# A list scheduler that writes four engine queues: scatters spaced on GpSimd, sums of y queued later, fewer zero products ahead of spreads, preparation due later

## The chip, the cores and the metric

The kernel runs on one core of a Trainium2 chip. Its engines are TensorE (PE, matrix products; PEld in the profile is its weight load), VectorE (DVE), ScalarE (ACT), GpSimd (POOL) and SyncE (SP, which only issues DMAs). Each works through its own queue in order; between queues there are only semaphores. GpSimd also issues indirect DMAs (gathers and scatters). The metric is the device time of one execution in microseconds, the median of several runs.

## The reference, cut to what matters

The program is four layers over an image batch of 4 x 64 x 64 x 96. Layers 2 and 3 (attention, an FFT layer and two quantised networks) and the second half of layer 1 are not touched. The work in question is the selective scan of layers 0 and 1. For each image and each of four scan directions, over 4096 positions, 192 channels d and 16 states n:

```python
# L1 (L0 is the same with other scan orders and weights)
x_dbl = einsum('bkdl,kcd->bkcl', xs, x_proj_w)       # dts, B, C
delta = softplus(einsum(dts, dt_projs_w) + dt_projs_b)
A = -exp(A_logs)
def step(h, (x_t, d_t, B_t, C_t)):
    h = h * exp(d_t * A) + (d_t * x_t) * B_t
    y = sum over n of h * C_t
```

In layer 0 the four directions are a diagonal snake, an anti-diagonal snake and two radial orders; in layer 1 they are rows and columns, forwards and backwards. The y of each direction goes back to image order and the four are added.

## The kernel before, in words

The scans of both layers are one stream of eight batches, one per layer and image: four of layer 0, then four of layer 1. A batch has 4 directions (kd) x 4 segments of 1024 positions, 16 segments. Between batches another stage (`side_by_side`) merges the finished image and projects a later one; its own planner is not part of the change. The first-layer norm, the projections and the layers after it stand outside too.

A segment is 24 groups: 6 blocks of 32 channels (cb) times 4 sets of 4 states (sg); a group is a tile of 128 partitions (32 channels x 4 states) x 1024 positions. For a group:

- `spread_u` (L1065, once per block): two products on TensorE copy 32 rows of dtu into all 128 partitions, into the one PSUM buffer u. It waits for the last product t of the block before.
- `load_dt` (L1056, once per block): SP loads dts, 512 KB, the same rows from DRAM, where L1020 has stored them. `load_states` (L1050) loads B and C, eight loads of 512 KB per segment, each into its one place in bc.
- `decay` (L1072): da = exp(dts * A) on ScalarE, four buffers.
- `enter` (L1076): t = u * B on VectorE.
- `recur` (L1083): the scan h on VectorE, four buffers. `keep` (L1094) copies its last column on ScalarE.
- `leave` (L1098): hc = h * C on GpSimd, three buffers.
- `collect` (L1107): TensorE adds hc over the states into y, two products.

VectorE's order is fixed: two products t, two scans h, and so on. After every two blocks y is copied (L1136), turned on TensorE (L1148) and copied into rows (L1152). At the end of a segment the rows are stored: in layer 0, directions 0 and 1, by eight scatters on GpSimd (`store`, L1162), each of 128 rows to scattered rows of the one DRAM tensor y_tok; else by SP. Directions 2 and 3 of layer 0 gather their input on GpSimd (L839); directions 0 and 1 load it in many small diagonal runs on SP (L835), and ScalarE copies it out in as many pieces (L913).

While a segment runs, the next one is prepared (`prepare`): x is turned on TensorE (L897) and copied (L908, L913), projected (L934), biased and split on ScalarE (L947, L949, L951, L953), softplus is made from exp and log (L991 to L1006), and dt is the sum of four terms, made on TensorE as four products with the identity into the one PSUM bank m (L1014), for two halves of the channels times two halves of the positions. ScalarE copies each sum out (L1017), which frees the bank for the next. When a half is complete, SP stores it to DRAM (L1020) and GpSimd multiplies it with x to dtu (L1023). The first spread of a segment needs the first half of dtu, its first decays the first dts load.

The order is written by a planner at build time. `Flow.run` takes the operations (`Op`) of a whole batch, each with an engine, a time on it (`occ`), a latency to users on other engines (`lat`), a due time, and perhaps `hard`. Due times are first lowered so that no user is late. Then it repeatedly takes the operation that can start soonest, and of those within 0.1 us the one with the earliest due time; an operation that isn't hard must not push the engine's next hard one (decay, spread, enter, recur, leave) past its due time by the planner's reckoning, unless its own due time is earlier. A user on the same engine is taken to be ready when the operation before it is done, without `lat`. What it writes is an order alone: on the chip each queue waits for semaphores, not for the planner's times.

When the planner sees a gap on TensorE it calls `keep_busy`, which puts in products with zeros (L1125) that add nothing to an open y:

```python
for _ in range(int((gap - 0.15) * 0.7 / 0.215)):
```

Of the kernel before, what the change touches and what calls it, by code (L numbers as in the profile page):

```python
# [29 lines left out]
SEG = 1024  # L30
# [12 lines left out]
class Kit:  # L43


    def __init__(self, tc, pool):
        self.tc, self.nc = tc, tc.nc
        nc = self.nc
        self.ident = self.t(pool, [128, 128], "ident")
        make_identity(nc, self.ident)  # L50
        self.eps = self.t(pool, [128, 1], "eps")
        nc.vector.memset(self.eps, 1e-5)
# [61 lines left out]
class Op:  # L114


    def __init__(self, engine, occ, emit, deps=(), lat=0.15, due=None, hard=False, bank=0, after=0.0):
        self.engine, self.occ, self.emit, self.lat = engine, occ, emit, lat
        self.deps = [d for d in deps if d is not None]
        self.due, self.hard, self.bank, self.after = due, hard, bank, after  # L120
        self.users, self.left, self.seen = [], 0, 0.0


class Flow:
# [11 lines left out]
    def run(self):  # L136
        inside = set(map(id, self.ops))
        for op in self.ops:
            op.deps = [d for d in op.deps if id(d) in inside]
            op.left = len(op.deps)  # L140
            for d in op.deps:
                d.users.append(op)
        for op in reversed(self.ops):
            for d in op.deps:
                due = op.due - d.occ - (0.0 if d.engine == op.engine else d.lat)
                d.due = due if d.due is None else min(d.due, due)
        free, ready, hard = {}, {}, {}
        for op in self.ops:
            free.setdefault(op.engine, 0.0)
            ready.setdefault(op.engine, [])  # L150
            if op.hard:
                hard.setdefault(op.engine, []).append(op)
        for ops in hard.values():
            ops.sort(key=lambda op: -op.due)
        for op in self.ops:
            if not op.left:
                ready[op.engine].append(op)
        bank, drift, left, strict = 0.0, 0.0, len(self.ops), True
        while left:
            best = None  # L160
            for engine, ops in ready.items():
                if not ops:
                    continue
                first = hard.get(engine, [])
                while first and first[-1].left < 0:
                    first.pop()
                when = lambda op: max(free[engine], op.seen, op.after, bank if op.bank > 0 else 0.0)
                fits = ops
                if strict and first:
                    limit = first[-1].due + drift - (3.2 if engine == "PE" else 0.5)  # L170
                    fits = [
                        op
                        for op in ops
                        if op.hard or op.due <= first[-1].due or when(op) + op.occ <= max(limit, free[engine])
                    ]
                    if not fits:
                        continue
                soonest = min(map(when, fits))
                if soonest == math.inf:
                    continue  # L180
                op = min((op for op in fits if when(op) <= soonest + 0.1), key=lambda op: op.due)
                if best is None or when(op) < best[0]:
                    best = when(op), op
            if best is None:
                assert strict
                strict = False
                continue
            strict = True
            start, op = best
            engine = op.engine  # L190
            if engine == "PE":
                self.fill(start - free[engine])
            op.emit()
            left -= 1
            op.left = -1
            ready[engine].remove(op)
            free[engine] = start + op.occ
            done = start + op.occ
            if op.bank:
                bank = math.inf if op.bank > 0 else done + op.lat  # L200
            if engine == "DVE":
                drift = max(0.0, start - op.due)
            for user in op.users:
                user.seen = max(user.seen, done if user.engine == engine else done + op.lat)
                user.left -= 1
                if not user.left:
                    ready[user.engine].append(user)
        return drift
# [168 lines left out]
class Stream:  # L377
# [493 lines left out]
    def prepare(self, seg, base=0.0, before=None):  # L871
# [3 lines left out]
        ops, o, b = [], seg.o, before.o if before else {}  # L875
# [1 line left out]
        chunks = [slice(j * CH, (j + 1) * CH) for j in range(SEG // CH)]  # L877

        def op(name, engine, occ, emit, deps=(), at=0.0, **kw):
            x = Op(engine, occ, emit, deps, due=base + at, **kw)  # L880
            ops.append(x)
            o[name] = x
            return x

        if seg.i == 0:

            def weights():
                seg.proj = k.t(self.seg, [C, 2, DI + 2 * NS], "proj", bufs=2)
                nc.sync.dma_start(seg.proj, lay.proj[kd])

            op("proj", "SP", 0.1, weights, [b.get(("P", 1, 1))], lat=4.0, at=2.0)
# [23 lines left out]
        for j in range(0, SEG // 128, 2):  # L915
# [5 lines left out]
            if seg.turned:  # L921
                for jj in range(2):
                    occ = 0.19 * len(seg.turned[j + jj]) + 0.25
# [32 lines left out]
        for half in range(2):  # L956
            for j in range(2):
                at = 20.0 + 3.5 * (2 * half + j)
                free = []
                if (half, j) == (0, 0):  # L960
                    free = [b.get(n) for n in (("u", 0), ("u", 1), ("out", 0), ("out", 1), "bc_out", ("sum", 1, 1))]
# [8 lines left out]
                    at=at,  # L970
# [54 lines left out]
        for half in range(2):  # L1025
            for j in range(2):
                at = 48.0 + 4.0 * (2 * half + j)
                for term in range(4):
# [6 lines left out]
                        at=at + 0.9 * term,  # L1035
                        lat=0.3,
# [4 lines left out]
            done = [o["dt", half, 0], o["dt", half, 1]]  # L1041
# [72 lines left out]
            )  # L1114
        self.open = gr if gr.sg < NSG - 1 else None

    def keep_busy(self, gap):


        gr = self.open  # L1120
        if gr is None:
            return
        at = gr.cb % 2 * GC
        for _ in range(int((gap - 0.15) * 0.7 / 0.215)):
            self.nc.tensor.matmul(  # L1125
                gr.seg.y[at : at + GC, :256],
                self.zeros,
                gr.seg.bt.lay.diag.rearrange("p h t c -> p (h t c)")[:, :256],
                start=False,
                stop=False,  # L1130
                tile_position=(0, at),
            )
# [21 lines left out]
    def store(self, seg):  # L1154

        nc, ops = self.nc, []
        rows = lambda: seg.rows.rearrange("p f t d -> p (f t) d")
        to = seg.bt.y_tok[seg.kd]

        def scatter(j):  # L1160
            at = seg.i * (SEG // 128) + j
            nc.gpsimd.indirect_dma_start(  # L1162
                out=to,
                out_offset=bass.IndirectOffsetOnAxis(ap=self.order[:, seg.kd, at : at + 1], axis=0),
                in_=rows()[:, j, :],
                in_offset=None,
            )

        def whole():
            at = self.start(seg)  # L1170
            dst = to[at : at + SEG, :].rearrange("(f p t) d -> p f (t d)", f=2, t=4)
            nc.sync.dma_start(dst, seg.rows.rearrange("p f t d -> p f (t d)"))

        def columns(w):
            nc.sync.dma_start(self.by_columns(to, seg, w), rows()[w * HW : (w + 1) * HW])

        if seg.bt.lay.ordered and seg.kd < 2:
            return [Op("POOL", 1.25, partial(scatter, j), lat=4.0) for j in range(SEG // 128)]
        if seg.bt.lay.ordered or seg.kd % 2 == 0:
            return [Op("SP", 0.1, whole, lat=4.0)]  # L1180
        return [Op("SP", 0.1, partial(columns, w), lat=4.0) for w in range(2)]
# [568 lines left out]
class Ffn:  # L1750
# [20 lines left out]
    def __call__(self, xs, store):  # L1771

        nc, take, give = self.k.nc, self.rings.take, self.rings.give
        xq = yield from take(self.work, [C, 4, CH], "xq", 2, F8)
        xm = yield from take(self.work, [C, 4, CH], "ln_xm", 1)
        read = []

        def out(j, rs):
            nc.vector.tensor_tensor(xq[:, j], xm[:, j], rs, ALU.mult, saturate=False)
            self.plan.add(self.layers(xq, j, xs[j], store, read))  # L1780

        yield from self.norm(xs, [xm[:, j] for j in range(4)], out)
        give(xm)
        del xm

    def layers(self, xq, j, x, store, read):
        nc, work, take, give = self.k.nc, self.work, self.rings.take, self.rings.give
        hq = yield from take(work, [128, 3, CH], "hq", 3, F8)
# [599 lines left out]
```

## Time and profile before

| | |
|---|---|
| median of 3 runs | 15374.65 us (15372.34 to 15387.42) |
| profiled execution | 15402.95 us, span 15401.2 us |
| mean granted clock of TensorE | 0.937 |
| eight scan batches | 386 to 1736, 1948 to 3279, 3492 to 4829, 5054 to 6380 us (layer 0); 6589 to 7891, 8051 to 9344, 9500 to 10801, 10900 to 12194 us (layer 1) |
| scans h, VectorE (L1083) | 2304 of 2355 ns and 768 of 2287 ns |
| products t, VectorE (L1076) | 3072 of 1239 ns |
| products hc, GpSimd (L1098) | 3072 of 2365 ns |
| decays, ScalarE (L1072) | 3072 of 1151 ns |
| zero products, TensorE (L1125) | 7824 records (two passes each), 1986.3 us |
| scatters, GpSimd (L1162) | 256 of 997 ns |

The page's first part gives busy time, share and instruction count of each engine over the whole span. A window view gives the same for a stretch of time, with the clock that was granted to TensorE as a share of full speed. A wait line reads: engine and line that stood idle, what it waited for; us in total, times, the longest. A timeline line starts with the start and the length in us. A product of f32 with 512 columns stands in the trace as two passes.

### The profile page before, as it was taken

What the parts mean: (1) busy time and instruction counts of PE and PEld (TensorE: products, weight loads), DVE (VectorE), ACT (ScalarE), POOL (GpSimd) and SP (SyncE); (2) the same over time, 40 slices, a digit from 0 to 9 for tenths busy, and PEclk for the clock granted to TensorE, in tenths of its full rate; (3) what the DMA queues carried; (4) which work ended last, traced back from release to release, by engine and by line L of the source; (5) the groups of instructions that cost most, each with busy time, mean ns of one, the idle gap of its engine ahead of it and who ended that gap; (6) DMA issues with size and microseconds to landing.
All of it is one profiled execution on the core that took longest, in us unless ns stands there. A gap on an engine that the chain in (4) does not pass through costs nothing. (4 is left out here: it accounts for less than half of the span.)

```text
span 15401.2 us, 196660 instructions
## 1 busy us (share of the span) xinstructions
PE 13827.4 (90%) x74369; PEld 5096.1 (33%) x74369; DVE 12827.4 (83%) x9642; ACT 8327.7 (54%) x13421; POOL 9203.3 (60%) x4657
## 2 busy tenths in 40 slices
PE   8899899989998999899989998999899789998877
PEld 3233333333333333333333333333233244443344
DVE  1999799978997899799979997999899856555655
ACT  3666466646664666466656665666566423232333
POOL 0788678867886688667747774777577620000123
PEclk9999899989998999899989999999999999998888
DMA  2333433343334333433343334333433400000122
GB/s 67 117 113 125 150 111 111 126 148 112 111 127 146 106 118 128 148 116 117 123 152 124 118 124 152 126 118 120 156 119 120 142 10 11 19 15 12 52 72 71
DMA packets 662768, 1637.49 MB, mean 106 GB/s; under 512 B 102822, under 2 KB 268460, under 8 KB 658045
## 3 DMA queue, kind: packets, MB, share of 16 engines
q1 hardware_dynamic: 624956, 1549.37, 31.4%
q0 software_dynamic: 36864, 75.55, 1.7%
q8 instruction: 588, 9.63, 0.3%
q14 instruction: 360, 2.94, 0.1%
HBM read 1295.03 MB, written 329.58 MB: 105 GB/s over the span
## 5 line engine op out<-in xcount | busy, mean ns | idle before, releaser
L1098 POOL TENSOR_TENSOR hc<-h,bc 128x1024 f32<-128x1024 f32 x3072 | 7198.4, 2365 | 2216.1 <-DVE h L1083 1909.0
L1083 DVE TENSOR_TENSOR_SCAN h<-da,state,t 128x1024 f32<-128x1024 f32 x2304 | 5300.4, 2355 | 26.0 <-ACT state L1094 16.3
L1072 ACT ACTIVATE da<-dts,L_A_logs 128x1024 f32<-128x1024 f32 x3072 | 3520.0, 1151 | 1832.2 <-DVE h L1083 1786.7
L1076 DVE TENSOR_TENSOR t<-u,bc 128x1024 f32<-128x1024 f32 x3072 | 3629.8, 1239 | 267.6 <-PE u L1065 193.5
L1107 PE MATMUL y<-hc,gather_y 128*32 128x512 f32 x12288 | 3529.1, 620 | 311.9 <-POOL hc L1098 241.7
L1125 PE MATMUL y<-L_diag,zeros 96*32 96x256 f32 x7824 | 1986.3, 386 | 0.0
L1083 DVE TENSOR_TENSOR_SCAN h<-da,t 128x1024 f32<-128x1024 f32 x768 | 1717.4, 2287 | 17.3 <-ACT da L1072 9.1
L1065 PE MATMUL u<-dtu,spread 32*128 32x512 f32 x3072 | 1573.1, 632 | 120.0 <-DVE t L1076 109.2
L1125 PEld LDWEIGHTS y<-L_diag,zeros 96*32 96x32 f32 x7824 | 852.8, 111 | 1425.0 <-issue 926.1
L1107 PEld LDWEIGHTS y<-hc,gather_y 128*32 128x32 f32 x12288 | 595.8, 109 | 2021.1 <-issue 1029.1
L934 PE MATMUL m<-xs,proj 96*128 96x512 f32 (+1 forms) x2048 | 1070.2, 641 | 67.3 <-ACT spare L1152 32.5
L1642 DVE SCALAR_TENSOR_TENSOR hcv<-padv,taps,hcv 128x2048 f32<-128x2048 f32 x384 | 902.2, 2350 | 13.4
L1566 POOL MEMSET padp<- 128x2448 f32 x32 | 68.6, 2143 | 1400.8 <-PE d L1606 1378.3
L1023 POOL TENSOR_TENSOR dtu<-dt,xs 96x1024 f32<-96x1024 f32 x256 | 603.0, 2356 | 506.1 <-ACT dt L1017 501.1
L1606 PE MATMUL d<-padp,diag 32*32 32x512 f32 x25600 | 885.7, 601 | 2.0 <-ACT hcp L1621 2.0
L1065 PEld LDWEIGHTS u<-dtu,spread 32*128 32x128 f32 x3072 | 521.4, 188 | 943.6 <-issue 588.0
L1017 ACT COPY dt<-m 96x512 f32<-96x512 f32 x512 | 297.2, 580 | 694.5 <-PE m L1014 690.0
L1014 PE MATMUL m<-dtu,ident 96*96 96x512 f32 x1024 | 563.8, 632 | 72.7 <-ACT dt L1017 65.9
L1606 PEld LDWEIGHTS d<-padp,diag 32*32 32x32 f32 x25600 | 484.4, 103 | 369.8 <-issue 196.9
L934 PEld LDWEIGHTS m<-xs,proj 96*128 96x128 f32 (+1 forms) x2048 | 324.6, 181 | 770.6 <-issue 483.8
L947 ACT ACTIVATE sp_z<-m,L_dtb 96x512 f32<-96x512 f32 x512 | 350.0, 684 | 409.5 <-PE m L934 393.5
L1014 PE MATMUL m<-sp_log,ident 96*96 96x512 f32 x1024 | 539.2, 608 | 0.0
(275 smaller groups left out, 15495.8 us busy)
## 6 DMA issues: line engine op xcount, KB each, us to landing
bc<-bc_dram SPq DMA_DIRECT2D x1024, 512.0 KB
dts<-dt_dram SPq DMA_DIRECT2D x768, 512.0 KB
dt_dram<-dt SPq DMA_DIRECT2D x256, 384.0 KB
y_tok<-spare SPq DMA_DIRECT2D x64, 768.0 KB
dt<-y_tok SPq DMA_DIRECT2D x128, 384.0 KB
x_tok<-y_rows SPq DMA_DIRECT2D x32, 768.0 KB
z_t<-z_rows SPq DMA_DIRECT2D x64, 384.0 KB
dx<-x_tok SPq DMA_DIRECT2D x64, 384.0 KB
```

Source lines behind the costliest of these rows:

```text
L934: nc.tensor.matmul(v.ps, seg.proj[:, src, to], seg.xs[:, src, chunks[j]], start=src == 0, stop=src == 1)
L1014: nc.tensor.matmul(v.ps, k.ident[:C, :C], term[:, half, chunks[j]], start=at == 0, stop=at == 3)
L1023: nc.gpsimd.tensor_mul(seg.dtu[:, half], v.dt[:, half], seg.xs[:, half])
L1065: self.nc.tensor.matmul(seg.u[:, cols], self.spread[rows, :], seg.dtu[rows, half, cols], start=True, stop=True)
L1072: self.nc.scalar.activation(gr.da, gr.seg.dts[gr.cb], AF.Exp, scale=scale)
L1076: self.nc.vector.tensor_mul(gr.t, gr.seg.u, self.bc[:, 0, gr.sg, :])
L1083: self.nc.vector.tensor_tensor_scan(gr.h[:, order], gr.da[:, order], gr.t[:, order], start, op0=ALU.mult, op1=ALU.add)
L1098: self.nc.gpsimd.tensor_mul(gr.hc, gr.h, self.bc[:, 1, gr.sg, :])
L1107: nc.tensor.matmul(seg.y[at : at + GC, :], self.gather_y, gr.hc[:, part * CH : (part + 1) * CH], start=gr.sg == 0, stop=gr.sg == NSG - 1, ...
L1125: self.nc.tensor.matmul(gr.seg.y[at : at + GC, :256], self.zeros, gr.seg.bt.lay.diag.rearrange("p h t c -> p (h t c)")[:, :256], start=Fal ...
L1606: nc.tensor.matmul(pc[i][j * 32 : (j + 1) * 32, :], diag[mine, ON_PE.index(t), tap, :], pad[mine, j * 8 + dy : j * 8 + dy + 8, dx : dx + H ...
L1642: nc.vector.scalar_tensor_tensor(to, win, wt, to, op0=ALU.mult, op1=ALU.add)
```

## The change

Five edits to the planner and what it is given; no operation is added or taken away but zero products.

1. Scatters: each now depends on the one before it and is marked `lands`: a user on the same engine also counts its latency, now 3.0 us (4.0 before).
2. Sums later: in the planner a user on TensorE of an operation on GpSimd (a `collect` of a `leave`) is ready 1.0 us later.
3. Zero products: ahead of a hard operation of TensorE (a spread), a gap is filled with a share of 0.35; ahead of others 0.7 as before.
4. Preparation: every operation of `prepare` is due 18.0 us later.
5. `keep_busy` takes the share.

```diff
-        self.users, self.left, self.seen = [], 0, 0.0
+        self.users, self.left, self.seen, self.lands = [], 0, 0.0, False
...
-                self.fill(start - free[engine])
+                self.fill(start - free[engine], 0.35 if op.hard else 0.7)
...
             for user in op.users:
-                user.seen = max(user.seen, done if user.engine == engine else done + op.lat)
+                pad = 1.0 if (engine, user.engine) == ("POOL", "PE") else 0.0
+                near = user.engine == engine and not op.lands
+                user.seen = max(user.seen, done if near else done + op.lat + pad)
...
         def op(name, engine, occ, emit, deps=(), at=0.0, **kw):
-            x = Op(engine, occ, emit, deps, due=base + at, **kw)
+            x = Op(engine, occ, emit, deps, due=base + at + 18.0, **kw)
...
-    def keep_busy(self, gap):
+    def keep_busy(self, gap, share):
...
-        for _ in range(int((gap - 0.15) * 0.7 / 0.215)):
+        for _ in range(int((gap - 0.15) * share / 0.215)):
...
         if seg.bt.lay.ordered and seg.kd < 2:
-            return [Op("POOL", 1.25, partial(scatter, j), lat=4.0) for j in range(SEG // 128)]
+            ops = []
+            for j in range(SEG // 128):
+                ops.append(Op("POOL", 1.25, partial(scatter, j), ops[-1:], lat=3.0))
+                ops[-1].lands = True
+            return ops
```

## The prediction

> **What bounds the kernel now.** I read the page first (one core, so no second die), then the engines' busy time in the eight scan batches, then VectorE's waits there, and last the timelines around single waits.
>
> ```profile
> PE 13827.4 (90%) x74369; PEld 5096.1 (33%) x74369; DVE 12827.4 (83%) x9642; ACT 8327.7 (54%) x13421; POOL 9203.3 (60%) x4657
> ```
>
> No engine is full over the whole span. The share is a mean over stages, so the scan batches have to be cut out. The windows below are the batches, four of layer 0 and four of layer 1; columns are us of window, busy us of each engine (instructions), granted clock, DMA.
>
> ```profile
> core 0: us, PE busy (x) PEld busy (x) DVE busy (x) ACT busy (x) POOL busy (x), PEclk, DMA share, GB/s
> 386.00:1736.00 1350.00, 1245.75 (x4070) 406.85 (x4070) 1291.53 (x768) 854.04 (x1498) 1097.32 (x543) 0.95 0.35 116
> 1948.00:3279.00 1331.00, 1235.68 (x4074) 404.73 (x4074) 1290.97 (x768) 851.57 (x1495) 1097.32 (x543) 0.96 0.35 115
> 3492.00:4829.00 1337.00, 1239.37 (x4074) 406.20 (x4072) 1291.04 (x768) 851.18 (x1495) 1097.51 (x543) 0.96 0.35 115
> 5054.00:6380.00 1326.00, 1225.71 (x4069) 400.69 (x4068) 1290.48 (x768) 849.20 (x1447) 1097.47 (x544) 0.97 0.35 116
> 6589.00:7891.00 1302.00, 1223.16 (x4102) 401.15 (x4099) 1289.99 (x768) 836.63 (x1211) 971.11 (x415) 0.98 0.36 118
> 8051.00:9344.00 1293.00, 1208.43 (x4099) 397.69 (x4098) 1287.73 (x768) 840.69 (x1214) 970.76 (x415) 0.99 0.37 119
> 9500.00:10801.00 1301.00, 1216.18 (x4102) 399.98 (x4102) 1289.10 (x768) 841.09 (x1215) 970.56 (x415) 0.98 0.36 118
> 10900.00:12194.00 1294.00, 1202.33 (x4124) 399.76 (x4124) 1287.96 (x768) 819.81 (x1186) 965.81 (x413) 0.99 0.36 117
> ```
>
> Here VectorE is the bound: 1288 to 1292 us of products and scans in every batch. Window minus VectorE busy is 58.5, 40.0, 46.0 and 35.5 us in layer 0 and 12.0, 5.3, 11.9 and 6.0 in layer 1: **215 us, all that this change can win**. The same subtraction over the first segment of each batch gives 44.6 us, a start-up the change hardly touches; 171 us are left. Outside the batches the diff changes no order.
>
> The waits say who holds VectorE up (total us, times, longest):
>
> ```profile
> POOL y_tok L1162 <- DMA y_tok<-spare,scan_idx: 123.5, 60, 4.6
> ...
> DVE t L1076 <- PE u L1065: 193.5, 123, 7.0
> ```
>
> VectorE's product t waits for the spread u on TensorE. Of the late spreads, those of layer 0 that stand right behind zero products or sums of y cost 83 us and those behind the last dt sum (L1014) 57 us; in layer 1 nearly all (26 of 29 us) stand behind zero products. The scatter's wait starts many of them: GpSimd stands 4.4 us behind its own scatter, the sums of y behind it stand, TensorE idles, and then its clock drops:
>
> ```profile
> 2047.10:2050.50 3.40, 2.50 (x7) 0.57 (x4) 3.40 (x3) 3.38 (x6) 0.00 (x0) 1.00 0.41 107
> 2050.50:2053.90 3.40, 1.98 (x4) 0.66 (x4) 3.40 (x3) 3.37 (x6) 2.84 (x2) 1.00 0.24 66
> 2053.90:2060.70 6.80, 5.84 (x11) 1.30 (x12) 6.80 (x5) 3.23 (x4) 4.96 (x5) 0.50 0.31 105
> ```
>
> Sorting TensorE's idle stretches in the batches by length: of 37 of 2.0 us or more, 35 were followed within 3.4 us by half clock, for about 7 us; of 756 under 1.5 us, 44 were.
>
> **The change part by part.** Instruction counts stay the same on every engine but TensorE.
>
> *Scatters.* In the old order 72 of the 224 follow-up scatters stand directly behind the one before and 4 behind one product; in the new order every one stands behind exactly two products hc, 2 x 2.365 = 4.73 us. A scatter lands 2.4 us (median) to 4.9 us (95%) after its issue, 1.0 of which is the issue itself. So the 123.5 us of GpSimd waiting go. It is off the bound; its worth is in the late spreads.
>
> *Sums later.* The added 1.0 us exists only in the planner. In the order, 95 of 96 spreads per batch now have four groups' sums still to come behind them (before: 47 in layer 0, 18 in layer 1; the others had three). A spread no longer stands behind the newest product of GpSimd. Who waits for that: hc has three buffers, so GpSimd may wait for a sum (108 us in all now); it has 1331 - 1097 = 234 us of slack a batch, so I put it at nothing.
>
> *Zero products.* 3912 become 3014; the 1004 right ahead of spreads go, 106 come elsewhere. 898 x 2 passes x 0.215 us = 386 us less on TensorE, none of it on the bound. The two ahead of a spread took 0.86 us; without them TensorE idles that long, which by the count above costs the clock seldom.
>
> I take these three to remove all 171 us. The bounds: 83 (only those behind zero products and sums in layer 0) and 171.
>
> *Preparation later.* This adds a wait. The dt sums of the next segment move from about 20 us ahead of its start to just ahead of its first spread: on TensorE the last four-term sum now stands directly, or with one sum of y between, in front of that spread. On ScalarE, at 12 of 15 boundaries in a layer-0 batch and 7 of 15 in layer 1, the first decay of the next segment now stands in front of the dt copy that frees the only PSUM bank m for that last sum. This decay needs the dts load; the load needs the dt store. The planner counts the load's 4.5 us but no time from the store to the load, since both are on SP. The trace does:
>
> ```profile
> SPq L1056 <- DMA dt_dram<-dt: 298.0, 117, 4.5
> ```
> ```profile
> 2515.24 0.31 SPq L1020 DMA_DIRECT2D dt_dram<-dt  x1
> 2518.32 0.51 SPq L1056 DMA_DIRECT2D dts<-dt_dram  x1
> ```
>
> In 16 such pairs: copy to store 0.03, store to load 3.08, load to its landing (semaphore increments in the trace) 3.65, together 6.8 us.
>
> The walk, in us before the moment at which VectorE could start the next segment (twelve pairs of groups, 6.735 us each, make the 80.8 us of a segment, 1293 / 16): the last spread's release, the end of the second product t of the tenth pair of groups, is at -(3 x 6.735 - 2.34) = -17.9 (two products take 2.34 in the timeline). Boundary A (24 in layer 0, 28 in layer 1): spread 1.72, a sum of y 0.9, one dt term 0.86, so -14.4; ScalarE is in a decay until -14.2; copy 0.58: -13.6; store and load 6.8: -6.8; decay 1.15 (row L1072): -5.7; copy 0.58: -5.1; four terms in eight passes 0.43 us apart, 3.5: -1.6; spread 1.98: +0.4. So 0.4 us late, and TensorE idles about 2.5 us before the last sum. Boundary B (segments 2 to 7 of a layer-0 batch, 24): all four terms follow the spread, so the copy ends at -11.2 and the first product is 2.8 us late; two bc loads of 512 KB stand right ahead of the store, worth 0 to 2 us more: I take 3.8, and 3 to 5 us of idle TensorE.
>
> Idle of that length brought half clock in 35 of 37 cases. Its price: the 1331 us batch at clock 0.96 has 8% of 1331 = 106 us of half clock and 40 us of idle VectorE, 0.38 us per us, so 2.6 us per stretch of 6.8 us. A: 0.4 + 0.9 x 2.6 = 2.7, x 52 = 140 us. B: 3.8 + 2.6 = 6.4, x 24 = 154 us. Bounds for both together: 0 (the copy is early enough) and 24 x 8.1 + 52 x 4 = 402 us.
>
> The Trainium skill, TensorE: Matmul & The Clock Gate, Part 1, says that the clock falls after at least one idle window of about 3.4 us. By that rule idle of 2.5 us at A would cost no clock, and the sum would be -171 + 52 x 0.4 + 154 = +4 us, an estimate; the 35 of 37 above speak against it.
>
> **Sum.** -171 + 140 + 154 = +123 us. The profiled run took 15402.95 (span 15401.2 and 1.8 around it), 28 above the median 15374.65, so 15526 there and **15498** as a median.
>
> **Rivals.** *1, faster:* the late preparation is hidden. If the first dt copy comes 1 us earlier than in my walk at A and 3.8 at B, the spread is ready in time and nothing pays for the 171 us. For it: 0.4 us at A is no more than a walk can miss. Against it: the walk gives the queues no delay of their own, and B is far off. With 0 to 40 us paid: 15205 to 15245. *2, in between:* the boundary waits come, but the clock holds: 52 x 0.4 + 24 x 3.8 = 112, minus 171 = -59: 15316; with half of the stretches at half clock (92 us more) 15408. Against it: the 35 of 37. *3, the change does not do what it says:* within a segment spreads stay late behind x turns and projections that wait for ScalarE; only 83 of 171 go: 15586. Against it: in segments 10 to 14 of layer 0 the same projections stand there and VectorE has at most 1 us of idle time in each.
>
> **How the numbers follow.** Forecast 0.46 (own range 15420 to 15590, 78 us below for A or B mis-sized, 92 above), rival 1 0.25, rival 2 0.18, rival 3 0.11. A measurement of this kernel tells about 0.2% (31 us) from no change. Of rival 2 I put 0.10 faster and 0.08 within 0.2%; two hundredths of the forecast lie there too. So faster 0.35, same 0.10, slower 0.55. The range runs from 15225, the middle of rival 1, to 15600, just past rival 3.
>
> **What would show it.** Right: scatter waits near zero on GpSimd; t waiting for u inside segments nearly gone; new waits of t for u at the first product of a segment, 2 to 8 us, with decay waiting for the dts load on ScalarE (now 2 times, then some 70) and the clock at 0.5 there; layer-1 batches slower than their 1293 to 1302 us. Wrong: decays never wait for dts, or wait and the clock stays full; then it is rival 1 or 2.

## The result, and the profile after

The changed kernel takes 15499.83 us (median of 7 runs, 15451.88 to 15516.9) against 15387.42 us of the kernel before in the same runs (15363.73 to 15415.73): 1.0068 times as long, 95% interval 1.0052 to 1.0083. Forecast were 15498 us, 123 us more than the median that the kernel before had at that time (15374.65); measured beside each other it is 112 us more. The total is right; several of the terms behind it are not, as the experiments show.

The profiled execution has a span of 15483.8 us and a mean granted clock of 0.910 (before: 15401.2 us and 0.937). The page's first part:

```profile
PE 13814.7 (89%) x72573; PEld 4962.3 (32%) x72573; DVE 12833.7 (83%) x9642; ACT 8282.6 (53%) x13421; POOL 9212.5 (59%) x4657
```

VectorE is as busy as before (12827.4 us), TensorE has 1796 instructions fewer. The eight scan batches, columns as in the prediction (us of window, busy us of each engine, granted clock, DMA):

```profile
core 0: us, PE busy (x) PEld busy (x) DVE busy (x) ACT busy (x) POOL busy (x), PEclk, DMA share, GB/s
373.00:1733.00 1360.00, 1235.13 (x3874) 390.73 (x3874) 1289.53 (x768) 850.82 (x1497) 1095.89 (x542) 0.92 0.34 115
1940.00:3296.00 1356.00, 1236.97 (x3881) 392.41 (x3882) 1289.81 (x768) 847.23 (x1494) 1096.43 (x542) 0.93 0.33 113
3500.00:4859.00 1359.00, 1238.50 (x3881) 392.99 (x3882) 1289.65 (x768) 847.13 (x1494) 1096.21 (x542) 0.93 0.33 113
5067.00:6423.00 1356.00, 1242.96 (x3877) 391.75 (x3876) 1289.80 (x768) 844.22 (x1446) 1095.72 (x542) 0.92 0.34 113
6626.00:7937.00 1311.00, 1226.77 (x3837) 382.01 (x3838) 1290.24 (x768) 827.13 (x1210) 967.36 (x413) 0.93 0.36 117
8097.00:9407.00 1310.00, 1219.19 (x3841) 381.52 (x3840) 1289.79 (x768) 833.28 (x1215) 968.80 (x414) 0.93 0.36 117
9565.00:10865.00 1300.00, 1210.70 (x3841) 379.51 (x3840) 1289.48 (x768) 833.33 (x1215) 969.00 (x414) 0.94 0.36 118
10970.00:12271.00 1301.00, 1207.28 (x3871) 383.32 (x3870) 1288.85 (x768) 812.55 (x1186) 966.56 (x413) 0.94 0.35 116
```

Window minus VectorE busy, added up, is 336 us; before it was 215. Sorted by place in the trace, some 306 us of it lie at the first product t of a segment (258 in layer 0, 48 in layer 1), 15 us in the first segments of the batches, 12 us inside the other segments. The layer-0 batches are all 1356 to 1360 us long (1326 to 1350 before): idle time has left the segments and gathered at their boundaries. The waits (us in total, times, longest), first one line of the kernel before, then the changed kernel:

```profile
ACT da L1072 <- DMA dts<-dt_dram: 32.2, 2, 30.0
```

```profile
DVE t L1078 <- PE u L1067: 348.8, 121, 11.2
ACT da L1074 <- DMA dts<-dt_dram: 340.6, 74, 30.2
```

The line of GpSimd waiting for its scatter (123.5 us before) is gone from the list. VectorE waits for the spread 348.8 us in place of 193.5, and the decay waits for the dts load 74 times in place of 2. One boundary of kind B, from the timeline (start, us, engine, line, operation; idle before it and what ended that):

```profile
2184.80 0.58 ACT L1019 COPY dt<-m 96x512 f32<-96x512 f32 x1 [1.68 <-PE m L1016]
2185.40 0.32 SPq L1022 DMA_DIRECT2D dt_dram<-dt  x1
...
2190.67 1.16 SPq L1058 DMA_DIRECT2D dts<-dt_dram  x2
...
2194.61 1.15 ACT L1074 ACTIVATE da<-dts,L_A_logs 128x1024 f32<-128x1024 f32 x1 [5.79 <-DMA dts<-dt_dram]
2195.66 0.56 ACT L1019 COPY dt<-m 96x512 f32<-96x512 f32 x1
...
2196.28 2.02 PE L1016 MATMUL m<-dtu,ident 96*96 96x512 f32 x2 [4.29 <-ACT dt L1019]
...
2201.18 1.02 PE L1016 MATMUL m<-sp_log,ident 96*96 96x512 f32 x2
...
2202.13 1.98 PE L1067 MATMUL u<-dtu,spread 32*128 32x512 f32 x4
...
2204.15 2.36 DVE L1078 TENSOR_TENSOR t<-u,bc 128x1024 f32<-128x1024 f32 x2 [8.81 <-PE u L1067]
```

It is the chain of the walk: copy, store, load, decay, the copy that frees bank m, the last dt sum, the spread, the product t. ScalarE stands 5.79 us at the decay with the copy behind it; TensorE then starts the sum after 4.29 us of idle time and needs 5.85 us from its start to the spread's.

```profile
2194.60:2198.00 3.40, 1.72 (x2) 0.68 (x3) 0.73 (x1) 3.39 (x4) 1.01 (x1) 0.50 0.90 341
```

The clock in that stretch is 0.50.

### The profile page after: what moved, and what is told of

Same layout as the page of the kernel before. It is cut to its first block, busy times and chain, and to the rows that moved or that the text cites. A ratio compares the mean times of both kernels' runs of the same rounds, so it can differ in the third digit from the quotient of the medians.

```text
span 15483.8 us, 192971 instructions
## 1 busy us (share of the span) xinstructions
PE 13814.7 (89%) x72573; PEld 4962.3 (32%) x72573; DVE 12833.7 (83%) x9642; ACT 8282.6 (53%) x13421; POOL 9212.5 (59%) x4657
## 5 line engine op out<-in xcount | busy, mean ns | idle before, releaser
L1078 DVE TENSOR_TENSOR t<-u,bc 128x1024 f32<-128x1024 f32 x3072 | 3595.2, 1216 | 422.8 <-PE u L1067 348.8
L1109 PE MATMUL y<-hc,gather_y 128*32 128x512 f32 x12288 | 3786.3, 664 | 28.4 <-POOL hc L1100 28.4
L1067 PE MATMUL u<-dtu,spread 32*128 32x512 f32 x3072 | 1659.7, 662 | 419.4 <-DVE t L1078 412.2
L1127 PE MATMUL y<-L_diag,zeros 96*32 96x256 f32 x6028 | 1508.1, 384 | 0.0
L1109 PEld LDWEIGHTS y<-hc,gather_y 128*32 128x32 f32 x12288 | 667.3, 114 | 1904.3 <-issue 1482.2
L1127 PEld LDWEIGHTS y<-L_diag,zeros 96*32 96x32 f32 x6028 | 620.4, 110 | 1011.0 <-issue 602.2
L1016 PE MATMUL m<-dt,ident 96*96 96x512 f32 x1024 | 556.4, 626 | 0.0
```

Source lines behind the costliest of these rows:

```text
L1016: nc.tensor.matmul(v.ps, k.ident[:C, :C], term[:, half, chunks[j]], start=at == 0, stop=at == 3)
L1067: self.nc.tensor.matmul(seg.u[:, cols], self.spread[rows, :], seg.dtu[rows, half, cols], start=True, stop=True)
L1078: self.nc.vector.tensor_mul(gr.t, gr.seg.u, self.bc[:, 0, gr.sg, :])
L1109: nc.tensor.matmul(seg.y[at : at + GC, :], self.gather_y, gr.hc[:, part * CH : (part + 1) * CH], start=gr.sg == 0, stop=gr.sg == NSG - 1, ...
L1127: self.nc.tensor.matmul(gr.seg.y[at : at + GC, :256], self.zeros, gr.seg.bt.lay.diag.rearrange("p h t c -> p (h t c)")[:, :256], start=Fal ...
```

## The experiments

The runs below were made on three other chips, four kernels at a time, each set beside its own runs of the kernel before (medians 15259.77, 15257.82 and 15262.07 us). The kernel before is thus about 127 us faster there than above. Times are compared as ratios within one chip; where two chips are set against each other it is said.

### The two kernels again, on one chip (e5, e6)

> The changed kernel itself, so that it stands beside the kernel before and the next kernels on one chip. Ratio to the kernel before 1.0052 to 1.0083 as measured, so +80 to +125 us; boundary waits of 280 to 310 us in all.

> The kernel before, for its profile on the same chip. If the 127 us by which it was faster on the chip of the first experiments lie between the scan batches, the eight batches add up to 10535 us within 20 and the stretches between them to 1120 to 1275 us, by the chip. If they lie in the batches, its late spreads cost less than 193.5 us there, and the 171 us that could be won were fewer on that chip.

The changed kernel: 15396.8 us, ratio 1.0084 (1.0071 to 1.0098), 139 us slower, a little more than the 80 to 125 expected; its boundary waits are 294 us. The kernel before: 15280.04 us in its one run. Its batches add up to 10566.4 us (10535.0 in the first profile, so 31 more and not within 20), and the seven stretches between them to 1118.8 us in place of 1273.3. So the 127 us lie between the batches (the single profiled run of e6 is itself 22 us above the median): each of the four stretches up to the first layer-1 batch takes about 175 us in place of 209 to 225. The changed kernel shows the same difference, a smaller one (179 to 185 here, 203 to 208 on the first chip). Why one chip does this work more slowly was not looked at. The idle time that could be won is there on this chip too: 245 us by the windows.

The two traces on this chip also show a cost of the change outside the scan windows. Of the 111 us between the two profiled runs 69 lie in the batches (10635.4 against 10566.4) and 38 in the seven stretches between them (1156.9 against 1118.8). With the later preparation dt sums for the next batch stand among the last instructions of a batch: the last turn of y ends 8 to 12 us after the last scan in place of 5 to 6, and VectorE starts on the merge after 16 to 22 us in place of 13 to 16, 28 us over the seven. (In e1 below, without the later preparation, it is 13 to 16 us as before.) On the first chip VectorE's start is late in the same way (23 us over the seven), but there the stretches as a whole were 26 us shorter than before.

### Without the later preparation (e1)

```diff
-            x = Op(engine, occ, emit, deps, due=base + at + 18.0, **kw)
+            x = Op(engine, occ, emit, deps, due=base + at, **kw)
```

> The changed kernel with the preparation due as before; scatters, sums of y and zero products as changed. Theory: these three remove the waits of t for u (193.5 us in the kernel before) and add no boundary wait, so 130 to 175 us faster than the kernel before (15210 to 15255 us, ratio 0.9885 to 0.9915), layer-0 batches near 1290 to 1300 us. Rival (they reach only the spreads behind zeros and sums of layer 0): about 83 us faster (15300). Rival (the boundary waits of the changed kernel come from the later sums or the missing zero products, not from the preparation): no faster than before.

15203.88 us, ratio 0.9965 (0.9953 to 0.9977): 56 us faster, not 130 to 175, and less than the rival's 83. There is no boundary wait to speak of (37 us), so the third reading falls. The late spreads sorted by what stands directly ahead of them on TensorE, against e6: behind zero products 85 us in layer 0 and 43 in layer 1 become none; behind the last dt sum of layer 0 61 become 59; behind sums of y, turns and projections, in both layers, 8 become 52. The scatters, the later sums and the zero products do not clear the segments by themselves. The late spreads behind the dt sums are still there, and they are not there in the changed kernel: it is the later preparation that takes the dt sums out of the segments and puts their wait at the boundary.

### Each of the three alone (e9, e10, e11)

Each is the kernel before with one edit of the change: the scatters' dependence and `lands`; the 1.0 us from GpSimd to TensorE; the share of 0.35.

> The kernel before with the scatters spaced apart and nothing else. Theory: GpSimd's waits for its own scatters (107 to 124 us) go, and with them the late spreads of the layer-0 segments in which scatters stand; 15 to 50 us faster, layer 1 (no scatters) within 20 us of before. Rival (the scatter's wait is hidden by GpSimd's slack): within 15 us of before although the waits are gone.

> The kernel before with the sums of y queued 1 us later and nothing else. Theory: a spread no longer stands behind the newest product of GpSimd, so the late spreads behind zero products get fewer in both layers (85 us in layer 0 and 43 in layer 1 on the chip of e6): 20 to 60 us faster; those behind the last dt sum (61 us) stay. Rival: the sums behind the spread are late instead and hold the next one, within 15 us of before.

> The kernel before with a share of 0.35 ahead of spreads and nothing else. Theory: two zero products fewer, 0.86 us, ahead of some 80 late spreads, so 20 to 60 us faster; half clock rises from some 640 to over 1000 us in the eight batches and costs nothing, since it falls where VectorE does not wait. If half clock had its price of 0.38 us per us, the kernel would be 100 us or more slower.

| kernel | median, us | ratio (95% interval) | t waits for u, us | half clock in the batches, us: layer 0, layer 1 |
|---|---|---|---|---|
| before (e6) | 15257.82 | 1 | 224.6 | 436, 204 |
| scatters alone (e9) | 15132.33 | 0.9919 (0.9905 to 0.9933) | 104.3 | 224, 170 |
| sums later alone (e10) | 15270.5 | 1.0007 (0.9998 to 1.0016) | 185.8 | 665, 718 |
| zero products alone (e11) | 15270.86 | 1.0007 (0.9998 to 1.0015) | 205.0 | 521, 394 |
| the three together (e1) | 15203.88 | 0.9965 (0.9953 to 0.9977) | 142.8 | 658, 700 |

The theory missed in all three, and at e10 the rival held. (At e11 half clock rose to 915 us and not to over 1000, and cost nothing that can be seen, as its theory had it: at 0.38 us per us the 275 us more would have been 105 us.) **The scatters alone give 130 us**, two and a half times the upper end that I gave them, and the other two give nothing alone and take away 74 us of the 130 when they are added (0.9919 to 0.9965, two chips). Windows of the second and third batch, first the kernel before (e6), then the scatters alone:

```profile
1903.00:3245.00 1342.00, 1244.26 (x4073) 406.14 (x4071) 1290.95 (x768) 849.57 (x1495) 1096.33 (x543) 0.96 0.34 114
3420.00:4761.00 1341.00, 1243.56 (x4077) 405.72 (x4078) 1291.04 (x768) 849.86 (x1495) 1096.91 (x544) 0.96 0.35 114
```

```profile
1876.00:3176.00 1300.00, 1226.99 (x4142) 406.01 (x4140) 1288.80 (x768) 850.40 (x1495) 1098.19 (x544) 0.98 0.36 118
3350.00:4650.00 1300.00, 1227.53 (x4145) 406.43 (x4144) 1288.83 (x768) 850.46 (x1495) 1097.66 (x543) 0.98 0.36 118
```

Forty us of VectorE's idle time go from each batch. In the waits, the line of e6 below has no counterpart in the run with the scatters alone:

```profile
POOL y_tok L1162 <- DMA y_tok<-spare,scan_idx: 107.4, 53, 4.6
```

The late spreads behind the last dt sum of layer 0 fall from 61 to 12 us, those behind zero products there from 85 to 23. The edit does not touch the dt sums, but a scatter that takes longer in the planner's timetable changes what it writes for the other engines. Ahead of the fifth spread of segment 2 of a layer-0 batch, TensorE's order is

```
before:         y, 7 zeros, y, 4 zeros, y, dt sum, dt sum, spread
scatters alone: y, 6 zeros, y, 3 zeros, dt sum, y, dt sum, spread
three together: y, y, 7 zeros, y, 3 zeros, dt sum, y, dt sum, spread
```

Is it the scatter's wait that made the spreads late, as the forecast had it, or this order? In segments 1 to 5 of the layer-0 batches (counted from 0) both changed, and 90 us of late spreads become none. In segments 6 and 7 TensorE's order stayed word for word; GpSimd's waits for its scatters (2 us in each) went, and the late spreads did not: 16.5 us before, 19.5 after; those behind the last dt sum of segment 6 are 1.51 to 1.52 us late in all four batches of both runs. And among the 20 segments 1 to 5 there are five in which GpSimd waited under 2 us for scatters in e6; late spreads cost 3.4 us in the mean in each of these, 4.9 in each of the other 15. By that some 68 of the 90 us (20 x 3.4) come from the order and 22 from the wait, an estimate; no run kept the order and took the wait away in these segments.

The later sums alone (e10) clear the spreads behind zero products in both layers (85 and 43 us to 0), and some 87 us return behind dt sums (61 to 88 in layer 0), sums of y, turns and projections. In the order with the three together, above, four sums of y stand between the two spreads and not three: the one that no longer stands ahead of the spread before has to be done as well. e1 has that order and no waits at scatters, and its dt sums are late by 59 us. That the fourth sum is the cause is argued from the order, not shown by a run that moves it alone. GpSimd's waits for sums of y, which the forecast put at nothing, rose too (hc has three buffers): from 115 us in e6 to 237 in e10 and 280 in e1. Whether any of that reaches VectorE was not tried.

The half clock stands against the price that I had put on it. Layer-1 windows, e6 and then e10:

```profile
6442.00:7742.00 1300.00, 1218.52 (x4102) 400.07 (x4099) 1289.53 (x768) 835.62 (x1211) 970.79 (x416) 0.98 0.36 118
7901.00:9205.00 1304.00, 1219.89 (x4103) 400.59 (x4102) 1289.47 (x768) 839.63 (x1215) 970.15 (x415) 0.98 0.36 118
```

```profile
6448.00:7741.00 1293.00, 1190.60 (x3720) 368.22 (x3718) 1289.63 (x768) 825.00 (x1211) 970.82 (x415) 0.93 0.37 118
7900.00:9194.00 1294.00, 1185.98 (x3716) 367.45 (x3716) 1288.86 (x768) 829.54 (x1214) 971.02 (x416) 0.94 0.37 119
```

The clock falls from 0.98 to 0.93 and the batches get shorter. Over the layer, 514 us more at half clock (718 against 204) go with 21 us less time (5189.3 against 5210.6). At 0.38 us per us they would have cost 195 us. VectorE's whole idle time in these four batches of e10 is 31 us, so 718 us at half clock can have cost no more than that.

### The later preparation alone (e2)

```diff
-            x = Op(engine, occ, emit, deps, due=base + at, **kw)
+            x = Op(engine, occ, emit, deps, due=base + at + 18.0, **kw)
```

> The kernel before with the preparation due 18 us later and nothing else. In its order the first decay of the next segment stands ahead of two dt copies at the boundaries into segments 1 to 8 of a layer-0 batch (32 in all), at none or one in the rest. Theory: each of these 32 costs what the changed kernel pays there, 7 to 10 us (mean 9 into segments 2 to 7), and the 57 us behind the last dt sum inside segments go: 32 x 8.5 - 57 = 215 us slower than before (15600), layer 1 within 20 us of before. Rival (the wait needs the other parts too): between -57 and 0 us against before.

15329.78 us, ratio 1.0052 (1.0038 to 1.0065): 70 us slower, a third of what I expected; layer 1 is as forecast (5170 us against 5211 in e6). In layer 0 (5427 against 5356) decays do wait for the dts load (174.7 us, 32 times, in place of 32.5, 2 times), but the first products t of the segments wait only 22 us: in this order the last dt sum stands behind the first spread of the segment, and it is the spread of the second half of the channels, 40 us into the segment, that comes late, by up to 9.2 us and 133 us in all. So the wait does not need the other parts, but where it falls and how large it is depends on them.

### The store seen by the planner (e3)

```diff
-            op(("out", half), "SP", 0.1, partial(out, half), done, at=60.0, lat=3.0)
+            op(("out", half), "SP", 0.1, partial(out, half), done, at=60.0, lat=3.0).lands = True
...
-                due = op.due - d.occ - (0.0 if d.engine == op.engine else d.lat)
+                due = op.due - d.occ - (0.0 if d.engine == op.engine and not d.lands else d.lat)
```

> The changed kernel, but the planner counts 3.0 us from the dt store to the dts load; then only the last dt copy, which nothing of the next segment waits for but dtu's second half, stands behind the decay. Theory (the decay that waits for the dts load holds the copy that frees bank m): the boundary waits nearly all go, 306 us of VectorE idle time down to under 60, so 250 to 290 us faster than the changed kernel and 140 to 180 us faster than before (15205 to 15250 us); t waits for u less than 80 us in all. Rival (the late dt sums are late by themselves, whatever stands on ScalarE): within 60 us of the changed kernel (15440 or more).

15213.04 us, ratio 0.9971 (0.996 to 0.9982): 47 us faster than before. Against the changed kernel (1.0084 on another chip) that is 1.1%, some 170 us, where 250 to 290 were expected and the rival had at most 60. The boundary waits fall from 294 (e5) to 119 us:

```profile
DVE t L1078 <- PE u L1067: 160.9, 84, 7.0
ACT da L1074 <- DMA dts<-dt_dram: 150.8, 67, 29.0
```

Decays still wait 67 times, but of the dt copies at most the last stands behind them, and no dt sum ahead of the spread waits for that one; most of their waiting costs nothing. Nor did the preparation simply move earlier: at the boundaries of kind B the store is issued 9.1 us before VectorE is free, in the changed kernel (e5) 9.2 us before, and yet the last dt sum starts 2.6 us before that moment in place of 0.8 us after it, and takes 3.8 us in place of 5.5. That shows the copy behind the decay to be the cause of the larger part. Of the 119 us left, 76 are at the 24 boundaries of kind B, 3.2 each: there four dt sums go through one bank, each behind the copy of the one before, and end up to 3 us after VectorE is free (1.2 in the mean). This part of the rival is true.

### The clock at the boundary (e4)

```diff
             if at == 0:
+                if (half, j) == (1, 1) and lay.ordered and 2 <= kd * NSEG + seg.i < 8:
+                    self.zeros_here(before, 8)
                 v.ps = k.t(self.ps, [C, CH], "m")
```

`zeros_here` puts eight products with zeros into the y that the segment before has still open (the sum of y before it keeps it open for them).

> The changed kernel with eight more zero products (3.9 us at full clock) in TensorE's idle time ahead of the last dt sum, at the boundaries into segments 2 to 7 of the layer-0 batches (24). The decay, the copy and the order stay. There TensorE stood idle 2 to 5 us, then went through the last sum at half clock, 6.9 us for eight passes that take 3.5 at full clock. Theory: the clock holds and each boundary gets 2 to 3.4 us cheaper, 50 to 80 us faster than the changed kernel, waits of 4 to 6 us stay. Rival (the wait alone counts, the half clock is only seen with it): within 20 us of the changed kernel. If the zero products run late, in place of idle time that is no longer there: up to 50 us slower.

15350.34 us, ratio 1.0063 (1.0049 to 1.0077); the changed kernel has 1.0084 on another chip, so about 32 us less, between the theory and the rival; the two intervals overlap, so the times alone don't prove a gain. The traces say it more sharply. The same boundary as above:

```profile
2172.67 1.15 ACT L1076 ACTIVATE da<-dts,L_A_logs 128x1024 f32<-128x1024 f32 x1 [5.93 <-DMA dts<-dt_dram]
...
2174.34 1.10 PE L1018 MATMUL m<-dtu,ident 96*96 96x512 f32 x2 [0.56 <-ACT dt L1021]
...
2176.99 1.02 PE L1018 MATMUL m<-sp_log,ident 96*96 96x512 f32 x2
...
2177.94 1.98 PE L1069 MATMUL u<-dtu,spread 32*128 32x512 f32 x4
...
2179.96 2.36 DVE L1080 TENSOR_TENSOR t<-u,bc 128x1024 f32<-128x1024 f32 x2 [6.71 <-PE u L1069]
```

The decay waits as long as before (5.93 us), TensorE idles 0.56 us in place of 4.29, and from the sum's start to the spread's it takes 3.60 us in place of 5.85. Over the 24 boundaries of kind B the last sum takes 3.60 us in place of 5.49 (e5), it starts 0.5 us later behind the zeros, and the product t is 6.94 us late in place of 8.34. None of the 24 sums runs into half clock any more (20 in e5). So the clock's share of the wait at B is 1.4 us of 8.3, 34 us in all; the rest is the chain itself.

### Less late, and the copy seen too (e7, e8, e12)

e7 and e8 are e3 with 12 and 6 us in place of 18; e12 is e7 with

```diff
-                op(("dt", half, j), "ACT", 0.5, partial(keep_dt, half, j), [p], at=at + 4.0, bank=-1)
+                op(("dt", half, j), "ACT", 0.5, partial(keep_dt, half, j), [p], at=at + 4.0, bank=-1, lat=1.5)
```

> Store latency seen by the planner as in e3, preparation due 12 us later in place of 18. In its order the last dt sum stands four to six instructions ahead of the first spread, and two of the three remaining copies behind a decay are gone. Theory (with the copy free of the decay, the 76 us left at the boundaries into segments 2 to 7 are the chain of four dt sums through one bank, simply too late): 6 us earlier takes most of them, the inside of the segments stays quiet: 30 to 80 us faster than e3, so 75 to 130 us faster than before. Rival (earlier sums are late inside the segment again, as in e1): equal to e1 or e3, 40 to 60 us faster than before.

> The same with 6 us. No dt copy stands behind a decay of the next segment; the last sum stands seven to eleven instructions ahead of the first spread. Theory: no boundary wait, but the last sums come near the last spread inside the segment, 13.5 us ahead of the boundary: 50 to 110 us faster than before, on either side of e7. Rival (the in-segment waits behind the last sum come back in full): 40 to 60 us faster than before, as e1.

> e7 (store latency seen, preparation due 12 us later), and the planner counts 1.5 us in place of 0.15 from a dt copy to its users, among them the next dt sum, which needs the bank. In e7 most late spreads stand behind the second term of a dt sum that waited for that copy on ScalarE (64 us). Theory: they fall to under 30 us and no boundary wait comes back: 20 to 60 us faster than e7, so 90 to 130 us faster than before. Rival (the sums then stand as a whole ahead of the spread and are late just the same): within 20 us of e7.

| kernel | median, us | ratio (95% interval) | boundary waits, us | late spreads behind dt sums, us |
|---|---|---|---|---|
| 18 us, store seen (e3) | 15213.04 | 0.9971 (0.996 to 0.9982) | 119 | 95 |
| 12 us (e7) | 15189.69 | 0.9954 (0.9942 to 0.9966) | 0 | 116 |
| 6 us (e8) | 15285.93 | 1.0016 (1.0005 to 1.0026) | 14 | 171 |
| 12 us, copy seen (e12) | 15125.83 | 0.9918 (0.9903 to 0.9933) | 6 | 49 |

(The last column counts those at the boundary too.) With 12 us no boundary wait is left, as expected, but the sums come late inside the segment: 68 us faster than before, not 75 to 130. With 6 us they fall ahead of a spread inside the segment in both layers, and all the gain is gone; the rival had put it at 40 to 60 us faster. Counting the copy's real delay (e12) gives 136 us, a little above the 90 to 130 expected: the late spreads behind the second term of a dt sum, 64 us of layer 0 in e7, fell to 3, those behind dt sums of any kind from 116 to 49. e12 and the scatters alone are the fastest kernels of the study, within their intervals equal, and both beat the two kernels of this case. Their edits can be joined; that was not run.

## Why the prediction was right, point by point

**The bound and what was to be seen** were as forecast. VectorE's busy time did not move (1289 to 1290 us a batch). The scatter waits are gone, waits of t for u inside the segments too (12 us), the new ones stand at the first product of a segment, decays wait for the dts load 74 times (some 70 forecast), and three of the four layer-1 batches are 7 to 17 us longer (the other is 1 us shorter). VectorE's idle time in the batches is 336 us; the forecast's own terms make 44.6 + 140 + 154 = 339. That the two agree so closely is in part luck: the first segments of the batches, which the forecast took as hardly touched, fell from 44 to 15 us (the later preparation does that: 17 in e5, 47 in e1), while 12 us stayed inside the segments and the boundaries took 306 us and not 294. And the diff does lengthen the ends of the batches, by 23 to 28 us (e5, e6), which the forecast had at nothing.

**The sum hides two errors of opposite sign.** "I take these three to remove all 171 us" failed: the three take 56 us (e1), which lies below the lower bound of 83. The scatters alone take 130, the later sums and fewer zero products give back 74 (on two chips). The bound was wrong because I sorted the late spreads by what stood directly ahead of them and took each class for a cause that an edit could remove. The classes are links of one order: an edit to GpSimd's scatters emptied the class of the dt sums, and an edit to the sums of y moved the time from one class to another. On the other side, the later preparation was charged 140 + 154 = 294 us on top of that; on top of the three it costs about 195 us (139 + 56, on two chips). By VectorE's idle time, e1 against e5, it adds 258 us at the boundaries (37 to 294), but it also takes 83 us out of the inside of the segments (91 to 8) and 30 out of the first ones, where it clears away the dt sums and what stands behind them, and I had credited that to the other parts; the stretches between the batches get 38 us longer (1119 to 1157). The mechanisms are the forecast's, the split between the parts is not, and that a charge of 294 where some 195 were due and a credit of 171 where 56 were due nearly cancel is luck.

**Boundary A** was forecast at 2.7 us, 52 times, and cost less: in the changed kernel's first profile 48 of the 96 boundaries that are not B have the waiting decay, and they are 1.6 us late in the mean, 77 us in all; the other 48 add 18. The walk was near. In us before VectorE is free, forecast and measured: store -13.6 and -12.8, load -10.5 and -9.6, decay -6.8 and -5.8, product t 0.4 and 1.6 late. The mis-sized term is the clock: I added 0.9 x 2.6 us to each, but TensorE idled 1.0 us ahead of the last sum in the mean and not 2.5, and that sum ran into half clock at 2 of the 96.

**Boundary B** was forecast at 6.4 us, 24 times, and is 8.8, 211 us. Here the walk was short at three steps: the store came at -9.4, not -11.2; from store to load passed 4.75 us, not 3.08; the decay started at -0.7 in place of -4.4. The last sum then took 5.8 us in place of 3.5, at half clock.

**The price of the clock** failed as a step. It came from dividing idle time by half clock in one batch, where both have a common cause. In the changed kernel half clock in the batches rises from 578 to 1506 us; by that price the difference alone would cost 353 us. It costs where a wait of VectorE ends behind TensorE, and there it costs the slower instructions: 1.9 us in the last sum of boundary B (e4). Elsewhere it is free or nearly so: at most 31 us for 718 us in layer 1 of e10. That the 294 us of the boundaries came out near the 306 measured is because the overcharge at A (140 against 95, all 96 boundaries that are not B taken in) and the shortfall at B (154 against 211) nearly cancel.

**When the clock drops** held up for the long stretches. In the batches of the changed kernel 77 of 78 idle stretches of TensorE of 2.0 us or more were followed by half clock within 3.4 us; in e10 82 of 86, in e9 18 of 23. The Trainium skill (TensorE: Matmul & The Clock Gate, Part 1) asks for at least one idle window of about 3.4 us; these runs disagree with it: of the 49 stretches between 2.0 and 3.0 us in the changed kernel 48 were followed by half clock. The other half of the count, that short idle time "costs the clock seldom", did not carry over: of TensorE's idle stretches of 0.15 to 1.5 us, 37 of 632 were followed by the start of half clock within 3.4 us in the kernel before, 158 of 521 in the changed one. The time did not suffer, because half clock costs so little where VectorE does not wait.

**The rivals.** Rival 1 (the late preparation is hidden) and 2 (the clock holds) did not happen. Rival 3's ground, that spreads inside the segments stay late, is true of the three parts alone, though they stand behind dt sums (66 us in e1) more than behind the turns and projections that it named (28); in the changed kernel the later preparation removes them.

## What to carry to other kernels

Where a planner writes the order, an edit to one engine's times acts through the orders of the others; a wait sorted by what stands directly ahead of it names a place in that order, and not what an edit will win. Such a planner should count the latency from a store to the load of the same data even when one queue issues both, and that of a copy which frees a buffer: with the first counted, the preparation could come 12 us later without a wait at the boundaries (e7), and with the second as well the late spreads behind dt sums inside the segments fell by more than half (e12). Each part of a change is worth running alone: here one edit of four held the whole gain, and the other three together turned 0.8% faster into 0.7 to 0.8% slower. And an edit to a stage can cost at its ends: here the tail of each batch, outside the windows that were looked at, grew by 3 to 4 us.

## What the runs showed of the hardware that was not expected

- Half clock of TensorE is free, or nearly so, where no one waits for it: in layer 1, 718 us of it in place of 204 with batches 21 us shorter and VectorE idle for 31 us in all (e10 against e6).
- Shorter idle stretches can drop the clock as well: in the changed kernel 141 of 239 between 1.0 and 2.0 us were followed by half clock, in e9, which has more zero products, 23 of 177. What else enters was not tried.
- From the issue of the dt store to the issue of the dts load that waits for it passed 3.2 us at boundaries A and 4.75 us at B, and another 3.7 to 3.9 us until the decay could start. At B loads of 512 KB are issued around it; that they are the cause is argued only.
- The kernel before took 34 to 49 us more in each of four stretches between batches on one chip than on another (first profile against e6), the changed kernel 22 to 28 us more. The medians of the kernel before agree within 5 us on that other chip and two more.
